# Four half-size gate products moved into the recurrences' last steps, and a work list of its own for the first two turns of the layers behind them

## The chip, the cores and the metric

The kernel runs on one core of one Trainium2 chip. That core has five engines with instruction queues of their own: PE (TensorE, matrix multiplications; its weight loads are shown apart as PEld), DVE (VectorE), ACT (ScalarE), POOL (GpSimd) and SP, which here only issues transfers (DMAs). Each engine works through its own queue in order and waits for the others through semaphores. The metric is the device time of one execution in microseconds.

## What is computed

The input `x` has 32 rows of 256 time steps with 256 features, and each row has a condition vector. Four layers follow, each added to its input:

```python
x = x + L0(cond, x)   # GRU over 256 steps: z, r = sigmoid(..); hh = tanh(xW + r*h U + ..)
x = x + L1(cond, x)   # recurrence: gate = sigmoid(h Wh + z Wz + b); h = tanh(h*leak + gate*z)
x = x + L2(x, cond)   # f, i = sigmoid(x W_f + b_f), sigmoid(x W_i + b_i); candidate = x W_c + b_c
                      # log f/(f+i) summed over time, exp, weighted sum over time
x = x + L3(x, cond)   # per row: gelu(x @ down_row) @ up_row, the matrices made from cond
```

Everything is in float32. L0 and L1 go step by step; L2 and L3 work on whole rows.

## The kernel before

**The recurrences.** A loop over t = 0 to 256 (L693) runs step t of L0 (`run0`) and step t - 1 of L1 (`run1`). On PE, step t has in this order: the product of `hT` with `w_urz`, whatever is due in the list `products`, the L1 product with `w_1z` (called `l_Wz` below, from the weight's name in the profile), the product `w_uh`, the L1 product with `w_1h` (`l_Wh`), and the projection of the next step. In step 256 only L1 is left: `l_Wz` and `l_Wh`. On ACT it has the sigmoids of `r` and `z`, the tanh `h1T` that finishes the L1 step before (`finish_1`, L681), the tanh of L0, the gate `gt` (L755), two scaled copies (L757), and what is due in `sigmoids`. POOL adds each finished L1 step into `X2` (`residual`, L688), the array of all rows in on-chip memory, shown as `X` in the profile. The last such addition, of step 255, ends the recurrences.

**The gates made meanwhile.** The L2 gates f and i of the first six of eight time slices of 32 steps (`NW_H` = 6, `CT` = 32) are made inside the recurrences, in units of one slice, eight rows and one half `e` of the features (`gate_unit`, L103). A unit multiplies into the tile `pg` (L378; one bank, the f half and the i half beside each other), ACT takes the sigmoids, DVE makes the sum `s` and the guarded product `g`, and SP stores s, i and g in DRAM. Dictionaries (`products`, `sigmoids`, `sums`, `transfers`) hold by step number what is due; `at` enters, `due` runs. The slices 6 and 7 are made after the recurrences, group by group.

**The last layers.** The 32 rows are eight groups of four. Each is carried through stages, one function per stage (`STAGES`, L918). A word such as `c:0` names a stage and a place in the group; `c:0@1` below is that word for group 1.

| word | function, line | engine | what |
|---|---|---|---|
| `lf` | late_gates, L794 | PE, ACT | slices 6 and 7 of f and i: 4 products of 256 columns, 2 sigmoids |
| `ls`, `lg` | L807, L810 | DVE | their sum and guarded product |
| `c` | candidate, L815 | PE | candidate, 2 products of 512 columns; two banks |
| `m` | weigh, L823 | DVE | candidate times i; frees the bank of `c` |
| `ln` | logs, L830 | ACT | two logarithms of two rows; `ln:1` has rows 2 and 3 |
| `sum`, `w` | L843, L853 | DVE | running sum of the logs, exponents |
| `exp` | L856 | ACT | three exponentials |
| `new`, `cum`, `h0` | L863 to L873 | DVE | weighting, sum over time, first state |
| `x` | add_hidden, L879 | POOL | adds L2 to the row in `X2` |
| `mid`, `last` | L898, L904 | PE (`mid` ACT too) | the two products of L3 |
| `y` | finish, L908 | DVE, SP | adds L3, stores the row, loads the matrices four rows on |
| `in` | fetch, L162 | SP | fetches one of g, s, i (0, 1, 2) of a group from DRAM |

The order of all words is written by hand in the string `TURN` (L926). A loop over ten turns runs it; each stage lags by a number of turns, so that one turn works on three groups, and words whose group does not exist yet or any more are left out. Every engine takes its words in that order. Tables of ACT's functions are loaded where the function set changes (1.28 us each in the trace). `in_s` and `in_g` have one buffer, so a group's fetches of them wait for the logarithms of the group before; `in_i` has one buffer for groups 0, 3 and 6 and two more for the others.

## Time and profile before

The runs of this kernel had a median of 955.35 us (three, 955.17 to 957.66). The profiled execution took 956.46 us; its span from the first to the last instruction is 954.6.

| stretch, us of the span | PE busy | DVE busy | ACT busy | clock of PE |
|---|---|---|---|---|
| 0 to 737.5, recurrences | 718.79 | 595.72 | 403.23 | 1.00 |
| 737.5 to 782.5, first turns | 38.65 | 36.31 | 35.13 | 0.96 |
| 782.5 to 913, full turns | 130.50 | 127.11 | 114.29 | 1.00 |
| 913 to 954.6, last turns | 31.42 | 29.30 | 19.69 | 0.92 |

A busy time is that in which the engine had an instruction at work. The clock is that granted to PE, as a share of full speed, averaged over the stretch. A releaser, written `<-`, is what ended an engine's wait. Matrix multiplications overlap their neighbours, so the time from one's start to the next is less than its own duration; where this text adds up durations it uses start to start.

### The profile page before, as it was taken

To read this page: it belongs to the slowest core of one execution; us is meant where nothing else is said; L and a number is where in the kernel's file an instruction comes from. 1 tells how busy PE (TensorE), PEld (TensorE's weight loads), DVE (VectorE), ACT (ScalarE), POOL (GpSimd) and SP (SyncE) were. 2 spreads that over 40 slices of the span, in tenths; PEclk is the share of its full clock that TensorE was granted. 3 is DMA by queue.
4 is the path that set the end of the run, shared out by engine and by line. 5 is a ranking of instruction groups with operands and counts; after the bars stand their busy time and mean duration, and the time that the engine had idled before them with its cause. 6 is when DMAs were issued, how large, how long until landed. Compare 5 with 4: busy or idle time off the path is not lost.

```text
span 954.6 us, 55121 instructions
## 1 busy us (share of the span) xinstructions
PE 919.4 (96%) x22806; PEld 630.6 (66%) x22806; DVE 788.4 (83%) x3409; ACT 572.3 (60%) x2648; POOL 236.5 (25%) x594
## 2 busy tenths in 40 slices
PE   7999999999999999999999999999998989999978
PEld 4666666666666666666666666666675557777756
DVE  5767788888888888888888888888776799999994
ACT  3455555555555555555555555555554788889972
POOL 1233322222222222222222222222222022222222
PEclk9999999999999999999999999999999999999989
DMA  8344212222222222222222222432241457777543
GB/s 265 108 126 147 79 51 92 65 73 92 70 92 77 92 66 67 91 70 90 69 86 76 65 97 66 131 119 83 73 128 54 122 165 230 224 228 224 188 158 117
DMA packets 104158, 107.71 MB, mean 113 GB/s; under 512 B 9153, under 2 KB 86241, under 8 KB 103906
## 3 DMA queue, kind: packets, MB, share of 16 engines
q1 hardware_dynamic: 103906, 104.18, 34.4%
q8 instruction: 179, 2.93, 1.3%
q14 instruction: 73, 0.60, 0.2%
HBM read 59.06 MB, written 45.09 MB: 109 GB/s over the span
## 4 chain that ended last, share of the span: by engine, by line
PE 80%; DVE 13%; ACT 3%; issue 2%; DMA 1%; POOL 0%; DVEq 0%; POOLq 0%; ACTq 0%
PE p L573 45%; PE ps_l L889 10%; PE pg L93 10%; PE ps_c L93 5%; DVE h L639 5%; PE p L600 3%; PE ps_g L93 2%; PE pw L489 2%; ACT other L657 2%; DVE hT L649 1%; ACT r L657 1%; DVE rh L725 1%; DVE cc L848 1%; DVE gate_g L138 1%; PE pw L429 1%
## 5 line engine op out<-in xcount | busy, mean ns | idle before, releaser
L573 PE MATMUL p<-w_W_rzh,xT 128*32 128x192 f32 x4096 | 214.8, 326 | 0.2 <-issue 0.2
L657 ACT ACTIVATE other<-p 128x32 f32<-128x32 f32 x512 | 74.2, 199 | 172.9 <-PE p L573 172.9
L639 DVE TENSOR_TENSOR_SCAN h<-other,keep 128x64 f32<-128x64 f32 x512 | 121.3, 278 | 66.3 <-ACT other L657 62.7
L573 PE MATMUL p<-w_U_rz,hT 128*32 128x128 f32 x4080 | 165.4, 279 | 6.0 <-DVE hT L649 0.2
L750 POOL TENSOR_TENSOR pairs<-xT,hT 128x64 f32<-128x64 f32 x256 | 82.2, 321 | 326.9 <-DVE other L766 273.6
L657 ACT ACTIVATE r<-p 128x32 f32<-128x32 f32 x510 | 72.8, 195 | 149.0 <-PE p L573 149.0
L689 POOL TENSOR_TENSOR X<-pairs,h1T 128x64 f32<-128x64 f32 x256 | 103.0, 402 | 214.9 <-DVE rhT L649 211.8
L573 PEld LDWEIGHTS p<-w_U_rz,hT 128*32 128x32 f32 x4080 | 97.4, 108 | 84.3 <-DVE hT L649 83.4
L639 DVE TENSOR_TENSOR_SCAN pre<-other,pairs 128x128 f32<-128x128 f32 x256 | 123.3, 481 | 34.2 <-ACT pairs L757 0.7
L573 PEld LDWEIGHTS p<-w_W_rzh,xT 128*32 128x32 f32 x4096 | 124.9, 110 | 22.4 <-issue 1.9
L573 PEld LDWEIGHTS p<-w_l_Wz,pairs 128*32 128x32 f32 x4096 | 79.2, 110 | 86.0 <-issue 69.2
L757 ACT ACTIVATE pairs<-h1T,leak 128x32 f32<-128x32 f32 x510 | 133.6, 314 | 0.4
L573 PE MATMUL p<-w_l_Wz,pairs 128*32 128x64 f32 x4096 | 120.3, 225 | 5.1 <-ACT keep L707 1.6
L573 PE MATMUL p<-w_U_h,rhT 128*32 128x64 f32 x4080 | 106.6, 221 | 0.4 <-issue 0.4
L573 PE MATMUL p<-w_l_Wh,h1T 128*32 128x64 f32 x4080 | 104.7, 219 | 0.8 <-issue 0.7
L725 DVE TENSOR_TENSOR rh<-r,h 128x32 f32<-128x32 f32 x510 | 74.9, 188 | 32.1 <-ACT r L657 5.7
L649 DVE STREAM_TRANSPOSE hT<-h 128x32 f32<-128x32 f32 x512 | 84.1, 198 | 0.0
L882 POOL TENSOR_TENSOR X<-X,w 128x512 f32<-128x512 f32 x32 | 41.4, 1306 | 165.3 <-DVE w L875 76.8
L649 DVE STREAM_TRANSPOSE rhT<-rh 128x32 f32<-128x32 f32 x510 | 80.0, 195 | 0.0
L573 PEld LDWEIGHTS p<-w_l_Wh,h1T 128*32 128x32 f32 x4080 | 76.4, 110 | 1.3 <-issue 1.0
L573 PEld LDWEIGHTS p<-w_U_h,rhT 128*32 128x32 f32 x4080 | 69.7, 108 | 5.5 <-issue 0.6
L686 ACT ACTIVATE h1T<-pre 128x64 f32<-128x64 f32 x256 | 69.5, 271 | 1.4 <-DVE pre L639 1.4
(108 smaller groups left out, 1470.5 us busy)
## 6 DMA issues: line engine op xcount, KB each, us to landing
adapted<-wm SPq DMA_DIRECT2D x128, 128.0 KB
wt<-adapted SPq DMA_DIRECT2D x28, 512.0 KB
xT<-in_xT_dram SPq DMA_DIRECT2D x32, 256.0 KB
w<-in_W_dram SPq DMA_DIRECT2D x32, 256.0 KB
out_dram<-y SPq DMA_DIRECT2D x32, 256.0 KB
gates<-gate_i SPq DMA_DIRECT2D x48, 128.0 KB
gates<-gate_s SPq DMA_DIRECT2D x48, 128.0 KB
gates<-gate_g SPq DMA_DIRECT2D x48, 128.0 KB
```

What stands on the lines that cost most here:

```text
L93: nc.tensor.matmul(ps[:, 0 : (h1 - h0) * (rows.stop - rows.start) * CT].rearrange("p (h b t) -> p h b t", h=h1 - h0, t=CT), w[:, k, e * P ...
L573: last = nc.tensor.matmul(ps[j * B : (j + 1) * B, cols], hT[:, k, :], w[:, k, j, :], start=False, stop=False, skip_group_check=True, tile_ ...
L639: nc.vector.tensor_tensor_scan(*(x[:, ns].rearrange("p n u -> p (n u)") for x in (done, other, pairs)), 0.0, ALU.mult, ALU.add,)
L649: nc.vector.transpose(dst[:, c], src[:, bass.ts(c, B)])
L657: nc.scalar.activation(dst[:, bass.ts(c, B)], src[:, bass.ts(c, B)], function)
L686: nc.scalar.activation(flat(h1T), pre, AF.Tanh)
L689: return nc.gpsimd.tensor_add(X2[:, :, :, s], by_chunk(pairs1.pop(s)[:, :, 0]), h1s.pop(s))
L725: rh_done = nc.vector.tensor_mul(rh[:, cs], r[:, cs], h[:, cs])
L750: nc.gpsimd.tensor_add(by_chunk(pairs1[t][:, :, 0]), x_of(t), hT)
L757: nc.scalar.activation(by_chunk(pairs1[s][:, :, 1])[:, c], h1T[:, c], AF.Copy, scale=leak[:, c : c + 1],)
L882: after(nc.gpsimd.tensor_add(x, x, ws[g][:, b]), on_vector)
L889: nc.tensor.matmul(ps[:, e, :], matrices[row][:, m, k, e * P : (e + 1) * P], src[:, k, :], start=(k == 0), stop=(k == NC - 1),)
```

## The change

Two things are changed. First, slice 6 of group 0's late gates is made inside the recurrences. Four products (for both feature halves e, f then i), each of 128 columns (four rows of 32 steps), go into `pg`: number 0 at step 255 with its sigmoid in that step; numbers 1 and 2 in `products` of step 256, the sigmoid of 1 right behind them; number 3 behind `l_Wh` of step 256; the sigmoids of 2 and 3 behind the last `finish_1`. `late_gates` then makes only slice 7 for group 0. Second, the first two turns take their words from a list of their own, `HEAD`, in which each word has its group. It has the same 64 words that those turns had, in another order; the turns from the third on are as before.

```diff
+    def first_late_gate(name, w, e, banks):
+        ps = banks[name][:, e * GB * CT : (e + 1) * GB * CT]
+        def multiply():
+            for k in range(NC):
+                gate_product(ps, w, e, k, slice(0, GB), NW_H, NW_H + 1)
+        def sigmoid():
+            if name == "f":
+                parts_f[0, e] = gu.tile([P, CB * CT], FP, name="gate_f", tag="gate_f")
+                dst = parts_f[0, e][:, 0 : GB * CT]
+            else:
+                dst = gated["i", 0][:, e, NW_H]
+            nc.scalar.activation(dst, ps, AF.Sigmoid, bias=vec("b_" + name, e))
+        return multiply, sigmoid
...
+        first_late = [
+            first_late_gate(name, w, e, {"f": pg[:, 0], "i": pg[:, 1]})
+            for e in range(NC) for name, w in (("f", w_f), ("i", w_i))
+        ]
+        at(products, T - 1, first_late[0][0])
+        at(sigmoids, T - 1, first_late[0][1])
+        for n in (1, 2):
+            at(products, T, first_late[n][0])
...
                 due(products, t)
+                if t == T:
+                    first_late[1][1]()
...
                     product(p_1[s], cols_1(s), h1T, w_1h)
+                if t == T:
+                    first_late[3][0]()
...
             finish_1()
+            for n in (2, 3):
+                first_late[n][1]()
...
     def late_gates(g, e):
+        hs = slice(NW_H + (g == 0), NH)
+        cols = slice((hs.start - NW_H) * GB * CT, (NH - NW_H) * GB * CT)
...
+    HEAD = """
+        in:2@2 lf:0@0 ls:0@0 lf:1@0 lg:0@0 c:2@0 c:1@0 ls:1@0 lg:1@0 ln:1@0 m:2@0 m:1@0
+        sum:2.1@0 sum:2.0@0 c:0@0 ln:0@0 m:0@0 w:2@0 sum:3.1@0 sum:0.1@0 in:2@1 in:1@1
+        sum:3.0@0 sum:0.0@0 sum:1.1@0 w:0@0 lf:0@1 lf:1@1 c:3@0 sum:1.0@0 ls:1@1 c:3@1 m:3@0
+        exp:0@0 in:0@1 w:1@0 m:3@1 new:0@0 exp:1@0 lg:1@1 ls:0@1 new:1@0 w:3@0 exp:2@0
+        cum:1@0 c:1@1 cum:0@0 h0:1.0@0 h0:0.0@0 exp:3@0 h0:1.1@0 lg:0@1 ln:1@1 x:1@0 ln:0@1
+        c:2@1 m:1@1 c:0@1 h0:0.1@0 in:1@2 x:0@0 m:2@1 m:0@1 in:0@2
+    """
     with tc.manual_schedule():
+        pieces = [(word, None) for word in HEAD.split()]
+        pieces += [(word, turn) for turn in range(2, NG + 2) for word in TURN.split()]
...
+            g = int(group[0]) if group else turn - ago
```

More of the change, by code (lines that the diff above doesn't have):

```diff
@@ L145, in gate_unit @@
         return multiply, sigmoid, add_up, guard, store
+    parts_f = {}
+    def first_late_gate(name, w, e, banks):
[11 more added lines that the diff above has]
+        return multiply, sigmoid
     gi = ctx.enter_context(tc.tile_pool(name="gates_in", bufs=1))
@@ L786, in group_tile @@
         return gp.tile([P, GB, NC, cols], FP, name=name, tag=name, bufs=bufs)
-    fs, ss, ccs, ws, pcs, parts_f = {}, {}, {}, {}, {}, {}
+    fs, ss, ccs, ws, pcs = {}, {}, {}, {}, {}
     mids, ys = {}, {}
@@ L798, in late_gates @@
             for k in range(NC):
-                gate_product(ps[:, gate], w, e, k, slice(g * GB, (g + 1) * GB), NW_H, NH)
-        dst = parts_f[g, e] = gu.tile([P, 256], FP, name="gate_f", tag="gate_f")
-        nc.scalar.activation(dst, ps[:, 0], AF.Sigmoid, bias=vec("b_f", e))
-        nc.scalar.activation(late(g, "i", e), ps[:, 1], AF.Sigmoid, bias=vec("b_i", e))
+                gate_product(
+                    ps[:, gate, cols], w, e, k, slice(g * GB, (g + 1) * GB), hs.start, NH
+                )
+        if g > 0:
+            parts_f[g, e] = gu.tile([P, 256], FP, name="gate_f", tag="gate_f")
+        nc.scalar.activation(
+            parts_f[g, e][:, cols], ps[:, 0, cols], AF.Sigmoid, bias=vec("b_f", e)
+        )
+        nc.scalar.activation(
+            late(g, "i", e)[:, cols], ps[:, 1, cols], AF.Sigmoid, bias=vec("b_i", e)
+        )
     def late(g, name, e):
@@ L932 @@
     """
+    HEAD = """
[6 more added lines that the diff above has]
+    """
     with tc.manual_schedule():
+        pieces = [(word, None) for word in HEAD.split()]
+        pieces += [(word, turn) for turn in range(2, NG + 2) for word in TURN.split()]
         tables, on_vector = False, None
-        for turn in range(NG + 2):
-            for word in TURN.split():
-                name, place = word.split(":")
-                f, ago = STAGES[name]
-                args = [int(n) for n in place.split(".")]
-                if name in ("new", "cum", "h0", "x") and args[0] < 2:
-                    ago -= 1
-                g = turn - ago
-                if not 0 <= g < NG:
-                    continue
-                if name in ("exp", "ln"):
-                    if not tables:
-                        nc.scalar.preload_act_table_set("natural_log_exp_and_others")
-                    tables = True
-                elif name in ("lf", "mid"):
-                    tables = False
-                on_vector = f(g, *args) or on_vector
+        for word, turn in pieces:
+            name, place = word.split(":")
+            place, *group = place.split("@")
+            f, ago = STAGES[name]
+            args = [int(n) for n in place.split(".")]
+            if name in ("new", "cum", "h0", "x") and args[0] < 2:
+                ago -= 1
+            g = int(group[0]) if group else turn - ago
+            if not 0 <= g < NG:
+                continue
+            if name in ("exp", "ln"):
+                if not tables:
+                    nc.scalar.preload_act_table_set("natural_log_exp_and_others")
+                tables = True
+            elif name in ("lf", "mid"):
+                tables = False
+            on_vector = f(g, *args) or on_vector
 def _laid_out(v):
```

## The prediction

> **What bounds the kernel now.** I read four views: the chain that ended last, the busy time by stretches, the order of work on PE and DVE around the place where the recurrences hand over, and the granted clock there by single microseconds.

> The chain, from the page: four fifths of the span is PE.

> ```profile
> PE 80%; DVE 13%; ACT 3%; issue 2%; DMA 1%; POOL 0%; DVEq 0%; POOLq 0%; ACTq 0%
> ```

> The stretches (columns: us, then busy us of PE, PEld, DVE, ACT, POOL, granted clock, DMA share, GB/s). From 750 DVE is full and PE has holes; from 790 PE is full. The last layers' two first turns are thus DVE's and the rest is PE's. What the change wins must be won before about 781 and is then carried by a full PE.

> ```profile
> 740.00:750.00 10.00, 10.00 (x30) 5.74 (x29) 3.81 (x8) 7.23 (x9) 0.00 (x0) 0.95 0.17 48
> 750.00:760.00 10.00, 8.16 (x28) 4.79 (x27) 10.00 (x19) 8.22 (x15) 0.00 (x0) 1.00 0.89 236
> ...
> 790.00:800.00 10.00, 10.00 (x48) 8.75 (x47) 9.62 (x16) 9.91 (x12) 1.59 (x3) 1.00 0.75 219
> ```

> PE in order of time (start, busy, what, idle before it and its releaser). The late gates of group 0 start when POOL's last residual ends (737.53). The line at 780.75 (`c:3@2`, the candidate unit 3 of group 2) is PE's last hole before its full stretch: I measure the change there.

> ```profile
> 737.58 2.08 PE L93 MATMUL ps_g<-X,w_W_f 128*128 128x256 f32 x4 [2.04 <-POOL X L689]
> ...
> 758.56 3.70 PE L93 MATMUL ps_c<-X,w_W_c 128*128 128x512 f32 x8 [1.84 <-DVE in_i L826]
> ...
> 766.83 3.72 PE L889 MATMUL ps_l<-X,wt 128*128 128x256 f32 x16 [2.85 <-POOL X L882]
> ...
> 780.75 1.98 PE L93 MATMUL ps_c<-X,w_W_c 128*128 128x512 f32 x4 [1.59 <-DVE in_i L826]
> ```

> DVE there: it waits for candidates one by one, begins its scans at 750.54, and later two `new` (L866) take 2.40 beside POOL's X, where two alone take 1.28.

> ```profile
> 749.87 0.75 DVE L826 SCALAR_TENSOR_TENSOR in_i<-ps_c,vecs,in_i 128x512 f32<-128x512 f32 x1 [0.97 <-PE ps_c L93]
> 750.54 3.59 DVE L848 TENSOR_TENSOR_SCAN cc<-f,s 128x256 f32<-128x256 f32 x6
> ...
> 766.60 2.40 DVE L866 TENSOR_TENSOR w<-in_i,w 128x512 f32<-128x512 f32 x2
> ```

> The clock. It falls to half inside 737 and is back at 741; the second time from 925.3 to 932.1. The stretches are 3.4 and 6.8 us, once and twice a unit of 3.4. Ahead of the first, PE had worked 25% of a unit; ahead of the second, none. A hole of 2.85 us (764.0 to 766.83) left it at 1.00.

> ```profile
> 737.00:738.00 1.00, 0.42 (x1) 0.42 (x2) 0.00 (x0) 0.05 (x1) 0.44 (x2) 0.79 0.00 0
> ...
> 740.00:741.00 1.00, 1.00 (x4) 0.82 (x3) 0.00 (x0) 0.00 (x0) 0.00 (x0) 0.51 1.15 334
> ...
> 925.00:926.00 1.00, 0.00 (x0) 0.00 (x0) 1.00 (x3) 0.97 (x3) 1.00 (x1) 0.65 0.00 0
> ...
> 932.00:933.00 1.00, 1.00 (x6) 0.90 (x5) 1.00 (x4) 0.10 (x1) 0.00 (x0) 0.93 0.03 8
> ```

> And the tile `pg`, in which the moved gates are made: PE waits for either sigmoid before it writes the other's half.

> ```profile
>   ACT gate_f L130: 1.4, 7
>   ACT gate_i L130: 1.2, 6
> ```

> **The change part by part.** The sum is made against the profiled execution (956.46, span 954.6), which stands 1.11 above the median of the runs, 955.35.

> *The recurrences' end.* Four half-size products come in: each 4 matmuls with 4 weight loads, and a 128x128 sigmoid. No trace line has a 128x128 weight with 128 columns. Above: a load lasts 0.19 alone. Below: 0.108, half of the 0.216 at which 256-column ones follow each other. Nearest are the 8 loads of L365 (128x128, 32 columns), 0.97 together: 0.12 each. The sigmoid lies between 128x64 (0.22) and 128x256 (0.46): 0.30. Product 0 sits in step 255 where full-size ones sat in other steps (those take 2.80 with, 2.79 without): nothing. Its sigmoid stands on ACT behind the copies that end at 733.94, so ends at 734.24. Products 1 and 2 write the same bank, wait for that, and run 8 x 0.12 to 735.27. In PE's order stand behind them `l_Wz` (ready at 734.54) and `l_Wh` (735.11), which everything after waits for: `l_Wh` starts at 735.51, 0.4 late. Sigmoid 1 ends before the gate `gt` that it stands ahead of on ACT; product 3 and sigmoids 2 and 3 fill holes. X ends at 737.93. Bounds: 0 if PE need not wait for sigmoid 0 (it is idle from 733.23), 1.1 with 0.19 per load and 0.2 for the hand-over. I take 0.4.

> *The late gates left.* 16 matmuls of 128 columns at 0.12: 1.94, where 16 of 256 took 5.39 at mostly half clock and would take 3.45 at full. From 734.3 PE now works 62% of the unit that ended at 737.6, more than the 46% of the unit 765.0 to 768.4 (counted on from 737.6), which kept its clock: full clock. [...]

> *The list.* I lay the new order out engine by engine, each word with its row's time, start to start: PE 1.73 for `lf`, `mid` and `last`, 1.72 for `c`; DVE 0.66 `m`, 0.60 `sum` and `new`, 0.59 `w`, 0.34 `ls`, 0.33 `lg`, 1.13 `cum`, 0.39 `h0`; ACT 1.28 a table load, 2.09 `ln`, 1.46 `exp`. The old order so laid out gives 766.80 and 780.4 for PE's lines at 766.83 and 780.75. In the new one PE has the gates by 739.9 and `c:2@0`, `c:1@0` by 743.4. ACT's first `ln` ends at 743.85. DVE starts `m:1@0` at 743.5 and its first sum at 744.16, not 750.54. From there it is never idle: 8 `sum`, 3 `m`, 4 `w`, 2 each of `ls`, `lg`, `new` and `cum` and 3 `h0`, 15.1 in all, bring it to `m:1@1` at 759.27. `new` no longer meets POOL's X (saves 1.1). PE meanwhile goes through 5 `c` and 2 `lf` (12.1) and stands at 755.4 before `c:0@1`, whose bank `m:1@1` frees: it starts at 760.05, a hole of 4.65. From there 9 words, 15.5, to `c:3@2`: 775.6, and its own wait for `m:0@2` gives 775.77. That is 4.98 ahead of 780.75.

> *SP's queue.* `in:2@2` goes ahead of `in:2@1`: group 1's gates come one fetch later (786 KB at about 300 GB/s: 2.6), near 745, for `m:3@1` at 752.4. `in:1@1` and `in:0@1` wait for `ln:0@0` as before. Nothing, unless a fetch had to wait 7 us.

> *The hole's clock.* 4.65 of nothing is nearer to the 4.97 at 921.3 (half clock) than to the 2.85 (none), and wherever the units fall, one has over two thirds of it. The clock comes back at the end of a unit full of work: 2.8 to 6 us of work at half, 1.4 to 3.0 lost. I take 2.0. [...] What is late then: `c:0@1` itself, so `m:0@1` and DVE behind it by 1.7.

> *The tail* keeps its order. Its hole fell badly in the profiled execution: 5.84 us of work at half, 2.9 lost, of a possible 1.4 to 3.1. I take 2.2 for an ordinary run: 0.7 less.

> Sum: 956.46 - 4.98 + 2.0 - 0.7 = 952.8, 0.27% under the median.

> **The rivals.**

> A. As summed, 952.8 (951.3 to 954.6 by the places of the units).

> B. The hole costs nothing, because DVE is early or a third of a unit's work keeps the clock (25% did not, 46% did): 952.8 - 2.0 = 950.8. For it: DVE's words are all short. Against: 15.1 us of them in a row.

> C. The wait for sigmoid 0 is dearer: with 1.1 instead of 0.4, and PE's work before 737.9 no longer spared, the gates run at half as before (+1.0 to 1.9): 954.5 to 955.4. For it: the wait is certain, its length not. Against: PE works more, not less, ahead of the gates.

> D. Slower: buffer order on SP. `in:2@2` takes the first of the pool's two `in_i` buffers, `in:2@1` the second. If the pool deals them out in rotation, `in:2@4` (turn 3) waits for group 2's last `new` (turn 4, about 817.7), and the outputs and matrices queued behind it on SP with it. `mid:1@2`, due at 817, then waits for 786 + 256 + 512 KB at 300 GB/s after a start of 1.2: about 6.4, and the clock after it: 952.8 + 7 = 960. It decides at the first fetch of turn 3. Against: in the trace no wait of a fetch is for a buffer that is taken while another is free; for: there all came free in the order taken, so it shows neither.

> **How the numbers follow.** 0.3% is 2.9 us, about what a measurement of this kernel can tell from no change; the line runs at 952.48, through A. A 0.50 (0.22 of it faster), B 0.22 (faster), C 0.13 (same), D with whatever else stalls 0.15. Faster 0.44, same 0.41, slower 0.15. The range holds A, B and C with their bounds, 949.8 to 956.5; A's own is 951.3 to 954.6.

> **What would show it.** Right: X's end at 737.9 and the L93 gates at 1.00 clock in under 2.2 us; the first L848 near 744; PE idle some 4.6 us before an L93 `ps_c` near 760, with half clock behind it; from 776 to 778 on PE full. Wrong: the first `l_Wh` of step 256 over 1 us late; a DVE hole between 744 and 759; no drop of the clock near 760; an SP wait of many us on L160 in turn 3.

## The result, and the profile after

The changed kernel ran at a median of 953.62 us (951.49 to 956.72, 22 runs) where the kernel before, run beside it, had 957.40 (955.17 to 959.26, 22 runs): a ratio of 0.9967, 95% interval [0.9958, 0.9976], so 0.33% faster. (The ratio is the estimate on record with this interval; the quotient of the two medians, 0.9961, lies inside it.) A second comparison, below, gave 0.9953. The profiled execution took 953.42 with a span of 951.6. The forecast was 952.8. The three runs of before that the forecast was set against (median 955.35) turn out to lie low in that kernel's spread.

From the page, the chain that ended last. PE's share went from 80 to 82%, DVE's from 13 to 11%, as one would expect if less of the first turns hangs on DVE.

```profile
PE 82%; DVE 11%; ACT 3%; issue 2%; DMA 1%; POOL 0%; SPq 0%; DVEq 0%; POOLq 0%; ACTq 0%
```

The same stretches as before (us, then busy us of PE, PEld, DVE, ACT, POOL, granted clock, DMA share, GB/s). DVE now works 8.79 of the first ten, not 3.81. PE's hole has moved forward and grown (5.55 busy in the second, 8.16 before), and the clock in it is 0.92.

```profile
740.00:750.00 10.00, 10.00 (x33) 6.00 (x32) 8.79 (x16) 9.24 (x11) 0.00 (x0) 1.00 0.76 207
750.00:760.00 10.00, 5.55 (x13) 2.21 (x12) 10.00 (x18) 7.68 (x15) 1.21 (x1) 0.92 0.24 63
790.00:800.00 10.00, 10.00 (x44) 8.00 (x43) 10.00 (x18) 9.85 (x14) 0.00 (x0) 1.00 0.88 267
```

PE in order of time. Product 1 waits 1.02 us for sigmoid 0; `l_Wh` of step 256 starts 2.76 after that of step 255 (2.29 in the kernel before, the first two lines). The 16 late gates run from 737.28 to 739.14, start to start 1.86 where they took 5.22 (737.58 to 742.80) before. The one hole is the 4.45 ahead of `c:0@1`; `c:3@2`, the second half of the line at 776.20, has no wait any more. Below I use the `mid` behind it (779.63) as a mark.

```profile
732.82 0.41 PE L573 MATMUL p<-w_l_Wh,h1T 128*32 128x64 f32 x16
735.11 0.43 PE L573 MATMUL p<-w_l_Wh,h1T 128*32 128x64 f32 x16
```

```profile
731.99 0.41 PE L601 MATMUL p<-w_l_Wh,h1T 128*32 128x64 f32 x16
733.41 0.71 PE L93 MATMUL pg<-X,w_W_i 128*128 128x128 f32 x4 [1.02 <-ACT gate_f L163]
733.96 0.61 PE L93 MATMUL pg<-X,w_W_f 128*128 128x128 f32 x4
734.50 0.43 PE L601 MATMUL p<-w_l_Wz,pairs 128*32 128x64 f32 x16
734.75 0.41 PE L601 MATMUL p<-w_l_Wh,h1T 128*32 128x64 f32 x16
...
737.28 0.68 PE L93 MATMUL ps_g<-X,w_W_f 128*128 128x128 f32 x4 [1.48 <-ACT in_i L163]
...
759.36 3.78 PE L93 MATMUL ps_c<-X,w_W_c 128*128 128x512 f32 x4 [4.45 <-DVE in_i L870]
...
776.20 3.60 PE L93 MATMUL ps_c<-X,w_W_c 128*128 128x512 f32 x8
779.63 3.62 PE L933 MATMUL ps_l<-X,wt 128*128 128x256 f32 x16
```

DVE there. The first sum starts at 743.56 (before 750.54). `m:1@1`, the L870 of 758.57 that frees the bank for `c:0@1`, comes at the end of 15 us without an idle moment; then DVE itself waits 2.17 for the candidate that PE makes at half clock.

```profile
743.56 1.28 DVE L892 TENSOR_TENSOR_SCAN cc<-f,s 128x256 f32<-128x256 f32 x2
...
758.57 0.74 DVE L870 SCALAR_TENSOR_TENSOR in_i<-ps_c,vecs,in_i 128x512 f32<-128x512 f32 x1
...
763.18 0.75 DVE L870 SCALAR_TENSOR_TENSOR in_i<-ps_c,vecs,in_i 128x512 f32<-128x512 f32 x1 [2.17 <-PE ps_c L93]
```

The clock by single microseconds. It stays at 1.00 behind the recurrences. In the hole it drops at 758.49 (half of that microsecond is at half clock, so its mean is 0.75) and is back at 765.32: 6.83 us at half, of which PE works the last 5.96. That is twice the 3.41 of the first stretch at half in the kernel before (737.57 to 740.98), which this text calls a unit. The clock's changes in one execution lie whole units apart: from 758.49 to the next drop at 922.33 it is 48 times 3.413, in the kernel before from 737.57 to 925.30 it is 55 times. The units below are counted on from such changes.

```profile
737.00:738.00 1.00, 0.72 (x6) 0.75 (x7) 0.00 (x0) 0.18 (x1) 0.25 (x2) 1.00 0.04 8
...
758.00:759.00 1.00, 0.00 (x0) 0.00 (x0) 1.00 (x3) 0.32 (x1) 0.21 (x1) 0.75 0.00 0
759.00:760.00 1.00, 0.64 (x1) 0.50 (x2) 1.00 (x2) 1.00 (x2) 1.00 (x1) 0.50 0.00 0
765.00:766.00 1.00, 1.00 (x5) 0.85 (x4) 1.00 (x2) 0.00 (x0) 0.00 (x0) 0.84 1.15 342
```

**A measure free of the recurrences.** POOL's last residual starts anywhere from 735.86 to 742.74 in the profiled executions below, though nearly all the work ahead of it is the same in all. So I split each execution: from the start of that residual (X) to the start of the marked `mid` (M), and from M to the end of the span. Before: X at 737.20, M at 782.57, span 954.6. After: 736.81, 779.63 and 951.6. "At half" is the time in which PE worked at half clock between X and M; half of it is lost (the four matmuls of `c:0@1` take 3.78 us at a clock of 0.50 here and 1.98 at 1.00 in pad_head_2), and the last column, an estimate, is X to M without that loss. own_banks and own_tiles have a single run each (957.40 and 951.94 us) and so no ratio.

| kernel | ratio to before, 95% interval | X to M | M to end | at half | X to M, full clock |
|---|---|---|---|---|---|
| before | 1 | 45.37 | 172.03 | 3.4 | 43.7 |
| the change | 0.9967 [0.9958, 0.9976] | 42.82 | 171.97 | 6.0 | 39.8 |
| the change again | 0.9953 [0.9939, 0.9968] | 41.80 | 171.44 | 3.4 | 40.1 |
| gates_only | 0.9969 [0.9955, 0.9982] | 42.12 | 171.26 | 3.3 | 40.5 |
| list_only | 1.0011 [0.9997, 1.0024] | 45.53 | 171.79 | 7.8 | 41.6 |
| pad_head | 1.0004 [0.9991, 1.0016] | 45.78 | 171.19 | 3.0 | (extra work) |
| pad_head_2 | 0.9935 [0.9916, 0.9953] | 40.10 | 172.14 | 0 | 40.1 |
| m_early | 0.9937 [0.9920, 0.9954] | 39.99 | 171.48 | 0 | 40.0 |
| m_early again | 0.9934 [0.9921, 0.9946] | 40.00 | 171.01 | 0 | 40.0 |
| m_early_pad_tail | 0.9920 [0.9903, 0.9937] | 39.98 | 170.75 | 0 | 40.0 |
| all_three | 0.9933 [0.9916, 0.9950] | 39.99 | 170.83 | 0 | 40.0 |
| own_banks | one run | 41.66 | 171.20 | 3.2 | 40.1 |
| own_tiles | one run | 41.75 | 171.49 | 3.4 | 40.0 |
| best | 0.9942 [0.9929, 0.9955] | 41.59 | 170.79 | 3.4 | 39.9 |

### The profile page after: what moved, and what is told of

It is laid out like the page before. It is cut to its first block, busy times and chain, and to the rows that moved or that the text cites. A ratio compares the mean times of both kernels' runs of the same rounds, so it can differ in the third digit from the quotient of the medians.

```text
span 951.6 us, 55155 instructions
## 1 busy us (share of the span) xinstructions
PE 920.9 (97%) x22822; PEld 632.4 (66%) x22822; DVE 788.1 (83%) x3409; ACT 573.4 (60%) x2652; POOL 236.0 (25%) x594
## 4 chain that ended last, share of the span: by engine, by line
PE 82%; DVE 11%; ACT 3%; issue 2%; DMA 1%; POOL 0%; SPq 0%; DVEq 0%; POOLq 0%; ACTq 0%
PE p L601 45%; PE ps_l L933 11%; PE pg L93 10%; PE ps_c L93 5%; DVE h L667 4%; PE p L628 3%; PE ps_g L93 3%; PE pw L509 2%; ACT other L685 2%; DVE hT L677 1%; ACT r L685 1%; DVE cc L892 1%; PE pg L115 1%; DVE rh L755 1%; DVE gate_g L138 1%
```

## The experiments

**The two parts of the change, each alone.** Theory: the gates are worth their half clock and the shorter chain behind them, the list pulls DVE's work forward but pays for its hole. In gates_only all turns take their words from the old list; in list_only all late gates of group 0 stay behind the recurrences.

```diff
 # gates_only
-        pieces = [(word, None) for word in HEAD.split()]
-        pieces += [(word, turn) for turn in range(2, NG + 2) for word in TURN.split()]
+        pieces = [(word, turn) for turn in range(NG + 2) for word in TURN.split()]
 # list_only: no first_late product or sigmoid, and
-        hs = slice(NW_H + (g == 0), NH)
+        hs = slice(NW_H, NH)
```

> The four moved gate products alone; the first two turns keep the old word order. Theory (the moved work keeps PE's clock up and halves the gates that are left): the gates after the last residual take about 1.9 us at clock 1.00, the last residual is 0.4 us later against its step, PE's hole at the first mid shrinks or moves 3 us earlier; time 2.5 us below before (2 to 4), ratio near 0.997. Rival (the gain of the change is the list's, the gates only shift work): within 0.5 us of before.

> The new word list alone; all late gates of group 0 behind the recurrences as before. Theory: the gates run at half clock after the recurrences as before (5.4 us for 16 matmuls), the hole of about 4.5 us before c:0@1 is there with half clock behind it; both losses together eat the list's gain: 0 to 2.5 us above before, at best 0.5 below. Rival (the list is what gains): 3 us or more below before, like the whole change.

The gates alone give about all that the whole change gives (0.9969 against 0.9967 and, in the second comparison, 0.9953; X to M 42.12 against 42.82 and 41.80), the list alone nothing that can be measured (1.0011, its interval reaching below 1). The trace says why. PE in list_only (start, busy, what, idle and its releaser): the late gates run slowly as before, and the list's hole comes on top.

```profile
738.06 2.08 PE L93 MATMUL ps_g<-X,w_W_f 128*128 128x256 f32 x4 [2.04 <-POOL X L713]
...
763.50 3.78 PE L93 MATMUL ps_c<-X,w_W_c 128*128 128x512 f32 x4 [4.45 <-DVE in_i L860]
```

At full clock, by the last column, the list alone would bring X to M from 43.7 to 41.6, and the second hole's clock takes 2.4 us, more than that. And gates_only holds the surprise. PE and the clock there: a hole of 2.85 us, which had left the clock alone in the kernel before, now drops it.

```profile
763.99 5.33 PE L933 MATMUL ps_l<-X,wt 128*128 128x256 f32 x16 [2.85 <-POOL X L926]
```

```profile
763.00:764.00 1.00, 0.01 (x1) 0.01 (x1) 1.00 (x3) 1.00 (x2) 1.00 (x2) 0.93 0.00 0
764.00:765.00 1.00, 1.00 (x2) 0.83 (x3) 1.00 (x2) 0.98 (x2) 1.00 (x1) 0.50 0.00 0
...
767.00:768.00 1.00, 1.00 (x5) 0.83 (x5) 1.00 (x3) 0.99 (x2) 0.00 (x0) 0.86 1.12 332
```

So the hole's length alone does not tell the two apart. Where the units fall does: in the unit that ended with this drop (760.45 to 763.86) PE worked 0.69 of 3.41 us, 20%; in the unit of before over its hole (764.88 to 768.29) it worked 1.46, 43%.

**Is it the clock, or the wait?** The hole of 4.45 can be filled or removed. pad_head fills it with 16 products of 256 columns that nobody reads; m_early keeps the work as it is and moves one word, `m:1@1`, up on DVE past six others (two `cum`, three `h0`, one `lg`), so that the bank comes free before PE needs it.

```diff
 # pad_head: pad makes 16 gate products of group 0's rows into a tile that nobody reads
-        c:2@1 m:1@1 c:0@1 h0:0.1@0 in:1@2 x:0@0 m:2@1 m:0@1 in:0@2
+        c:2@1 pad:2@1 m:1@1 c:0@1 h0:0.1@0 in:1@2 x:0@0 m:2@1 m:0@1 in:0@2
 # m_early
-        cum:1@0 c:1@1 cum:0@0 h0:1.0@0 ...
-        c:2@1 m:1@1 c:0@1 h0:0.1@0 ...
+        c:1@1 m:1@1 cum:1@0 cum:0@0 h0:1.0@0 ...
+        c:2@1 c:0@1 h0:0.1@0 ...
```

> The whole change, and 16 matmuls of 256 columns (3.5 us) whose result nobody reads, put on PE into the hole ahead of c:0@1; no other word moves. Theory (the clock): c:0@1 starts at the same place but runs its 4 matmuls in 1.9 us instead of 3.8 at clock 1.00; the hole has no half clock behind it; time 2 us (1.4 to 3.0) below the changed kernel, 5 to 6.5 below before, ratio about 0.994 to 0.995. Rival (behind the hole DVE sets the pace, the clock costs nothing): as the changed kernel, 0.9967.

> The whole change with m:1@1 put ahead of cum:1@0 in the list, so that c:0@1's bank is free 3.7 us earlier. Theory: PE's hole before c:0@1 falls from 4.5 to about 1 us and a hole of about 1.6 opens before mid:1@0, neither with half clock behind it; time 2 to 3 us below the changed kernel, ratio about 0.993 to 0.995. Rival (DVE sets the pace): the hole closes but the full stretch of PE begins where it began with the change at full clock or later; within 0.5 us of the changed kernel, 0.9967.

pad_head missed, and by a fault of the experiment: its filler read group 0's rows, to which POOL was just adding (`x`), so the filler itself waited and made a hole of 5.21, with 3 us at half behind it and 3.5 us of useless work.

```profile
760.14 2.07 PE L93 MATMUL ps_g<-X,w_W_f 128*128 128x256 f32 x4 [5.21 <-POOL X L926]
```

m_early gave 0.9937. Its PE: no wait over 1.6 us, and no microsecond from 735 to 780 below full clock.

```profile
756.43 1.98 PE L93 MATMUL ps_c<-X,w_W_c 128*128 128x512 f32 x4 [0.70 <-DVE in_i L870]
...
761.71 3.72 PE L933 MATMUL ps_l<-X,wt 128*128 128x256 f32 x16 [1.57 <-POOL X L926]
...
768.54 1.99 PE L933 MATMUL ps_l<-mid,wt 128*128 128x256 f32 x8 [1.38 <-ACT mid L946]
```

But m_early removes wait and half clock together. pad_head_2 is pad_head with rows that no engine writes at that time (group 7's): it leaves the chain of waits through DVE as it is and takes away the idle time alone.

```diff
-                    gate_product(ps[:, gate], w, 0, k, slice(0, GB), NW_H, NH)
+                    gate_product(ps[:, gate], w, 0, k, slice(r0, r0 + GB), NW_H, NH)  # r0 = B - GB
```

> The filler again, with the rows of group 7, which no engine writes in this stretch, in place of group 0's rows: the filler can now start as soon as PE is done with c:2@1. Theory (the clock): PE works 3.5 of the 4.5 us ahead of c:0@1; c:0@1 starts where it did and takes 1.9 us instead of 3.8, no half clock between 738 and 780; time 2 us (1.4 to 3.0) below the changed kernel, ratio to before 0.9935 to 0.9955. Rival (behind the hole DVE sets the pace, so that the clock costs nothing): 0.9967 as the changed kernel.

Ratio 0.9935. PE: the filler runs from 758.70 to 762.3, and `c:0@1` starts when DVE lets it, 22.55 us behind X as in the change. What is gone is the half clock.

```profile
758.70 1.03 PE L93 MATMUL ps_g<-X,w_W_f 128*128 128x256 f32 x4
...
763.31 1.98 PE L93 MATMUL ps_c<-X,w_W_c 128*128 128x512 f32 x4 [0.99 <-DVE in_i L870]
```

X to M is 40.10 with the filler, which keeps the wait, and 39.99 with the word moved, which shortens it: as long as the clock holds, shortening this wait gains no more than 0.1 us. m_early does not rid PE of idle time: it still stands idle for 4.2 us between X and M (4.9 in the change), in smaller waits for DVE, POOL and ACT (0.70, 1.57 and 1.38). So what both edits win over the change is the half clock, as two different edits show that agree to 0.1 us. What an order with no such waits at all would win, no run here shows.

**The tail's hole.** The filler also fits into the hole at 921 (4.97 us), ahead of a `mid` near the end.

```diff
 # on top of m_early
+        at_tail = pieces.index(("last:0", 8))
+        pieces.insert(at_tail + 1, ("pad:2@7", 8))
```

> m_early with the same filler, on group 0's rows, behind last:0 of turn 8, where PE has had a hole of 4.97 us in every trace. Theory (the clock): the hole falls to 1.5 us, no half clock between 905 and 945; 16 products behind it in 3.5 instead of 5.2 to 6.9 us; time 2.2 us (1.4 to 3.1) below m_early's 950.0, and runs that lie closer together. Rival (the tail is DVE's or POOL's): as m_early, 0.9937.

The forecast of 2.2 us (1.4 to 3.1) was missed. The clock is at 1.00 from 913 to the end of the matrix work, but M to end is 170.75, against 171.48 and 171.01 in the two executions of m_early. Over the eleven executions that keep the hole the mean is 171.55 (171.01 to 172.14), over the three that fill it 170.79 (170.75 to 170.83): 0.76 us, where the eleven lose 1.7 to 3.1 to the half clock (PE works 3.4 to 6.1 us at half there). PE there: it now comes too early for POOL's additions, and two waits of 1.5 us for them stand in its place.

```profile
924.53 3.72 PE L933 MATMUL ps_l<-X,wt 128*128 128x256 f32 x16 [1.51 <-POOL X L926]
...
933.16 3.72 PE L933 MATMUL ps_l<-X,wt 128*128 128x256 f32 x16 [1.46 <-POOL X L926]
```

**The wait for sigmoid 0.** The prediction put it down to the two halves of `pg` being one bank. own_banks gives each of the four moved products a bank of its own within one tile of four banks, `late`; all_three joins that with m_early and the tail's filler.

```diff
 # shortened
-            first_late_gate(name, w, e, {"f": pg[:, 0], "i": pg[:, 1]})
+            first_late_gate(name, w, e, late[:, n, 0 : GB * CT])   # n = 0 to 3, one bank each
```

> The whole change, but each of the four moved products has a bank of its own, which the recurrences no longer use then, in place of pg. Theory (products 1 and 2 wait for sigmoid 0 on account of pg's one bank): product 1 follows l_Wh of step 255 at once, PE's wait of 1.02 us for gate_f is gone, and l_Wh of step 256 starts 2.3 us behind that of step 255 as before the change, not 2.76; the end of the recurrences 0.4 us earlier against that step. Rival (the order on PE or ACT delays it, not the bank): 2.7 us or more between the two.

> m_early with the filler at the tail and the banks of their own: 0.4 us below m_early_pad_tail if the parts add up, near 947.5, ratio 0.9905 to 0.992. If the 0.4 is swallowed (the first turns are set by DVE words that do not start earlier), the same as m_early_pad_tail.

The wait stayed as it was, in a bank that nothing else used:

```profile
739.34 0.71 PE L93 MATMUL late<-X,w_W_i 128*128 128x128 f32 x4 [1.02 <-ACT gate_f L161]
```

So the bank is not what orders them. all_three then holds the same work and the same wait as m_early_pad_tail; its 0.9933, outside the 0.9905 to 0.992 expected, beside 0.9920 shows what two such figures can differ by for nothing. The next guess was the tile: own_tiles makes products 1 and 2 in `late` and leaves 0 and 3 in `pg`.

> The change, with the products 1 and 2 in a second tile of on-chip accumulators instead of in pg; 0 and 3 stay in pg. Nothing else differs. Theory (PE waited for sigmoid 0 because both lay in one tile): the wait of 1.02 us ahead of product 1 is gone, and l_Wh of step 256 starts 2.3 us after that of step 255, as in the kernel before (2.29), not 2.76. Rival (the eight small products themselves hold l_Wz up, wait or no wait): 2.6 or more. The time would be 0.45 us less than the change's by the first and the same by the second, which one time can't tell.

In its PE the wait is gone, and `l_Wh` follows 2.30 after its predecessor, as in the kernel before (2.29):

```profile
732.58 0.41 PE L610 MATMUL p<-w_l_Wh,h1T 128*32 128x64 f32 x16
732.92 0.71 PE L93 MATMUL late<-X,w_W_i 128*128 128x128 f32 x4
...
734.88 0.43 PE L610 MATMUL p<-w_l_Wh,h1T 128*32 128x64 f32 x16
```

So in these runs the order between a write and an earlier read went by the tile, the buffer that the program names: the write waited 1.02 us for the reader of another part of the same tile, in the same bank (the change) and in another (own_banks), and had no wait in a tile of its own (own_tiles). That cost 0.46 us.

**All together, on one chip.** The change, m_early, and m_early with the tail's filler and the two tiles (best).

> The change itself, on this chip, beside the next two kernels: 0.9967 with an interval of about 0.001 to either side, if chips differ in level alone.

> The change with m:1@1 nine words earlier on DVE, again, on the chip of the change: theory (the hole's half clock and part of the hole are what the change's list lost) 3 us below the change, ratio 0.9937. Rival (the first reading was a good chip): less than 1 us below it, 0.996.

> m_early with the two remedies together: 16 unread products of 256 columns behind last:0 in turn 8 (the tail's hole), and products 1 and 2 in a tile of their own. Theory (each loss was real and they add up): the tail gains about 2.2 us, the end of the recurrences 0.45: 2.6 below m_early_again, ratio 0.991. Rival (the tail's half clock is covered by what follows on DVE and the stores): at most 0.5 below it, 0.993.

The change 953.51 us, m_early 951.34, best 952.14, before 957.50. The change's 0.9953 lies outside the 0.001 around 0.9967 that was expected, though the two intervals overlap. m_early (whose expectation says nine words where DVE's are six) repeats its first figure and lies 2.2 us below the change beside it, where 3 were expected (the change came out better here than the first time). best adds nothing, so the remedies do not add up. PE and its clock in best show one reason: the late gates run at half clock again.

```profile
739.74 1.00 PE L93 MATMUL ps_g<-X,w_W_f 128*128 128x128 f32 x4 [1.53 <-POOL cc L900]
```

```profile
739.00:740.00 1.00, 0.26 (x2) 0.29 (x3) 0.00 (x0) 0.59 (x3) 0.44 (x2) 0.97 0.00 0
740.00:741.00 1.00, 1.00 (x7) 1.00 (x7) 0.00 (x0) 0.00 (x0) 0.00 (x0) 0.50 0.25 54
```

Its X to M of 41.59 is 1.6 longer than m_early's 40.00, about half of the 3.4 us at half. PE's idle time ahead of the gates, 1.53, is the same in own_tiles, where the gates ran at full clock: the units fell otherwise. Whether own tiles make the drop likelier can't be said from two executions. The simplest version that beats both kernels is m_early.

## Why the prediction was right, by its steps

- **The recurrences' end, +0.4 within 0 to 1.1.** `l_Wh` to `l_Wh` went from 2.29 to 2.76: +0.47. The products pace 0.14 per instruction there (0.55 for 4) and 0.116 among the late gates (16 in 1.86), around the 0.12 taken. The reason given, one bank, was wrong: the wait of 1.02 us stayed with a bank of its own (own_banks) and was gone with a tile of its own (own_tiles). (The working has 0.06 too much: 734.24 and 0.97 make 735.21, not 735.27.)
- **The late gates left, 1.94 at full clock.** 1.86, at 1.00. The share of work that the prediction compared with, 46%, is 43% on the trace's own units, and the unit across X's end in the change has 57%: the conclusion holds. In the other executions with the gates moved it was full clock too, except in best: the half clock that rival C feared exists, in one of twelve, but there without the dearer wait that was to cause it.
- **The list.** Counted from the end of X, 737.14 where the prediction had 737.93: first sum foretold at 6.23, measured 6.42; `m:1@1` 21.34 and 21.43; `c:0@1` 22.12 and 22.22; the hole 4.65 and 4.45. At full clock `c:3@2` was to start 4.98 early against the old line, 0.4 of it already spent on the recurrences' end, so 5.4 behind X. X to M went from 45.37 to 40.0 at full clock: 5.4. But this one term holds the gates' clock as well as the list, and the working does not part them: gates_only, with the old list, already has 42.12, or 40.5 at full clock.
- **The hole's half clock, 2.0 within 1.4 to 3.0.** Lost in the four executions that have the change's list and hole: 3.0, 1.7, 1.6 and 1.7, a mean of 2.0. The profiled one has the dearest. The 2.8 to 6 us of work at half were an estimate; these four show 3.2 to 6.0. What the trace of before shows of the clock's return: it came at 740.98 and at 932.13, each time behind a unit that PE filled to 100%, and not at 928.71, behind one that it filled to 72%.
- **SP's queue, nothing.** Nothing stuck in turn 3: its `in_i` was fetched from 795.53, 22 us before the end of group 2's `new` that rival D had it wait for (817.7), so it did not wait for that group's buffer, and rival D fell. By what rule buffers are handed out was not tried.
- **The tail, −0.7.** The executions with this hole have a mean M to end of 171.55, 0.5 below the 172.03 of before's profile. The size holds, but it is no effect of the change: the changed kernel's own profile has 171.97, as much as before. And of the "2.9 lost" not all can be won: with no half clock at all only 0.76 comes back, and PE then waits for POOL's additions.
- **Rival B** (the hole costs nothing) was refuted by all four executions. Its time of 950.8 is about what m_early brought.
- **The place of the line at 0.3%.** The first ratio is 0.33% and the second 0.47%; the forecast had the likeliest case straddle 0.3%. The parts give −2.9: +0.47, and X to M from 45.37 to a mean of 42.0. Of the 3.04 between the two profiled executions, 0.8 was there before `l_Wh` of step 255 (732.82 and 731.99), up to where both kernels do nearly the same.
- **Where luck helped.** The change's own terms, -4.98 and +2.0, make 2.98 us, 0.31%, near the 0.33 and 0.47% measured. That the time came out within 0.8 us of the forecast is in part chance: an ordinary run of the kernel before was taken as 956.46 - 0.7 = 955.8 and measured 957.40, 1.6 more, while the two medians lie 3.78 apart, 0.8 more than the terms. The two misses partly cancel.

What the prediction did not see is that the two halves of the change are not additive: at full clock the list is worth about 2 us alone (43.7 to 41.6) and about 0.5 behind the gates (40.5 to 40.0), and in both cases a hole's clock takes it back.

## What to carry to other kernels

Where PE runs ahead and then waits for another engine as it does here (2.85 us in gates_only, 4.45 in the change, 4.97 in the tail), cost the clock behind the wait apart from the wait: here the slow clock cost 1.6 to 3.0 us, and moving one vector instruction six words forward removed it, while shortening the wait gained no more than 0.1. Before filling every such hole, look at what comes next: the tail's hole gave back 0.76 of 1.7 to 3.1, with POOL close behind. And split the measurement where the changed part begins, since the time of the part ahead varied by more than the change was worth.
